# Layer 0 of a two-layer Mamba kernel: B's diagonals made on GpSimd for both units, one softplus burst a block, two conv tiles activated out of PSUM, lead times given state by state

## The chip, the cores and the metric

The kernel runs on one NeuronCore of a Trainium2 chip. The metric is the device time of one execution in microseconds (us), less is better. The engines are named as in the profile: PE is TensorE (matmuls and transposes), PEld its weight loads, DVE is VectorE, ACT is ScalarE, POOL is GpSimd, SP is SyncE, which here only issues DMAs. Each engine works through its own queue in order. An instruction at the head of a queue that waits holds up everything behind it.

## What is computed

The input `x` has the shape (2, 64, 64, 256). Layer 0 adds to it a bidirectional Mamba over rows and over columns; layer 1 adds two rounds of Mamba-2 (along both axes). Everything is fp32. The change is in layer 0 alone, whose core is this:

```python
def mamba(x, in_proj_w, conv_w, conv_b, x_proj_w, dt_w, dt_b, A_log, Dp, out_w):
    xz = x @ in_proj_w.T
    xi, z = jnp.split(xz, 2, axis=-1)
    ...
    xi = jax.nn.silu(conv(xi) + conv_b)                # depthwise, 4 taps, 512 channels
    x_dbl = xi @ x_proj_w.T
    dt, Bm, Cm = jnp.split(x_dbl, [DT_RANK, DT_RANK + D_STATE], axis=-1)   # 16, 16, 16
    dt = jax.nn.softplus(dt @ dt_w.T + dt_b)
    A = -jnp.exp(A_log)
    dA = jnp.exp(dt[..., None] * A)
    dBu = (dt * xi)[..., None] * Bm[:, :, None, :]

    def step(h, t):
        dA_t, dBu_t, C_t = t
        h = dA_t * h + dBu_t
        return (h, jnp.einsum('ndk,nk->nd', h, C_t))
    ...
    y = y + xi * Dp
    y = y * jax.nn.silu(z)
    return y @ out_w.T
```

For each of 512 channels and 16 states, `h` is a linear recurrence along a sequence of 64 positions, driven by `dt * xi` times B, and read out by a sum over the states weighted with C. It runs forwards and backwards, over the rows (`mh`) and the columns (`mv`) of the image.

## The kernel before

**Tiling.** A block is four sequences of 64 in both directions: V = 512 positions in the free dimension, with channels on the 128 partitions. There are 16 blocks an axis, two axes and two images, hence 64 blocks (`Block`). The 512 channels are two units `u` of UC = 2 tiles of 128. For each unit and each of 16 states `n`, in one turn of 32 a block:

- `decay` (L744): ACT writes exp(dt * A), two instructions of 128x512.
- `inflow` (L765): dt * x * B of this state, made in one of three ways, which the string `B_BY` (L172) picks by state:
  - G: POOL multiplies `dtx` by a row of B that a DMA has spread over all partitions (`b_row`). The decay then lies in PSUM (`ps_h`), the inflow in SBUF (`b`).
  - T: ACT scales the transposed `dtxt` by B, a column now, into `scaled` (`prepare`, L753, four instructions), and PE transposes it back into `ps_h` (eight). The decay lies in `b`.
  - P: `prepare` makes diagonal matrices of B (`diag`) from the identity, in four ACT instructions, and PE multiplies `dtxt` by them into `ps_h`, with eight matmuls.
- `scan` (L780): DVE runs the recurrence over 1024 columns, into SBUF (`prod`) if POOL makes the product with C, else in place in `ps_h`.
- `times_c` (L795): the product with C's spread row (`c_row`), on POOL for the states in `POOL_C` (L176), else on DVE.
- `add` (L805): PE transposes the product eight times, accumulating into `ps_y`, the unit's sum over states.

**Buffers.** `ps_h` has two buffers, `prod` three, `b` three, `b_row` three, `c_row` four, `scaled`, `dtxt` and `diag` one each; `ps_mm`, PSUM for all projections, conv and transposes back, has two. `ps_y` has one.

**Around the states.** For each block, PE makes the input projection (`x_proj`), the conv as four diagonal matmuls for each tile and direction (`conv`), then the projections to dt, B and C (`bc_proj`) and to dt's channels (`dt_proj`). ACT copies or activates them (`x_copy`, `conv_copy` L645, `silus` L650, `dt_softplus` L711). `bc_spread` (L664) writes B and C to DRAM and issues all the row loads of the block on SP's queue, each waiting for its buffer. `dt_x` (L718) is POOL's product dt * x, after which dt is set to a huge value at the starts of sequences, so that the decay there is 0. `y_copy`, `y_back`, `gated`, `out_proj` and `residual` finish a unit or a block.

Silu and softplus lie in other activation tables than exp, so ACT loads a table before each burst of them and another to come back.

**What sets the order.** Nothing is scheduled by a compiler: `pin` keeps the program's order on each engine. Every step has a time by hand: `STEPS0` (L40) for the steps of a block, `LEADS` (L174) for the states' steps, in hundredths of a turn. `plan` (L269) shifts the list by one period for each block, and `issue` (L282) sorts all of it and records the instructions in that order. So work for later blocks stands between the states of this one. The times only fix the order; the engines then run as their semaphores let them.

## Time and profile before

| what | us |
|---|---|
| median of 3 runs | 8563.11 |
| lowest, highest | 8562.77, 8568.54 |
| the profiled execution's own time | 8561.29 |
| its span, first to last instruction | 8559.5 |

The profile is of one execution; between its span and the time of that execution lie 1.8 us. The mean granted TensorE clock was 0.967.

Busy time of the engines by stage, from the view by windows (us of the span):

| stretch | PE | PEld | DVE | ACT | POOL |
|---|---|---|---|---|---|
| 1000 to 2000, layer 0 | 899.3 | 763.8 | 959.1 | 843.9 | 989.1 |
| 4000 to 5000, layer 0 | 900.0 | 765.9 | 962.9 | 846.0 | 993.8 |
| 6600 to 7600, layer 1 | 1000.0 | 792.0 | 727.3 | 782.5 | 721.2 |

Layer 0 takes the span up to about 6240, layer 1 the rest. A group row of the profile reads: line, engine, operation, what it writes and reads, shape, count | busy time, mean ns of one | idle time of the engine just before, and what ended it. A timeline row reads: start, duration, engine, line, operation, how many in a row, and in brackets the idle time before. Lines such as L467, L470 and L474 are those of the helpers `act`, `matmul` and `transpose`, so that groups are told apart by tile names.

### The profile page before, as it was taken

The page shows a single profiled execution, that of the slowest core. Times are in us where ns is not written, and L with a number is a line of the kernel's source. Part 1 is how long each engine was busy: PE and PEld are TensorE (multiplying, and loading weights), DVE is VectorE, ACT ScalarE, POOL GpSimd, SP SyncE. Part 2 cuts the span into 40 slices and gives each one's busy share as a digit, 9 for nine tenths or more (in the row PEclk, how much of TensorE's full clock was granted, in tenths as well). Part 3 has the DMA queues.
Part 4 walks back from the last instruction along what each step waited for, and adds up shares of the span by engine and source line. Part 5 has one row for each costly group of instructions (what it writes and reads, how often), then busy time and mean ns, then how long its engine had stood idle before and what let it go on. Part 6 is the DMA issues. An engine that isn't in the chain of part 4 may idle for free. (4 is left out here: it accounts for less than half of the span.)

```text
span 8559.5 us, 150239 instructions
## 1 busy us (share of the span) xinstructions
PE 7881.5 (92%) x55632; PEld 6562.3 (77%) x55632; DVE 7631.3 (89%) x7371; ACT 7022.7 (82%) x12082; POOL 7776.3 (91%) x4490
## 2 busy tenths in 40 slices
PE   7989999899989889999998999899889999999999
PEld 6777777777777777777777777777667777777777
DVE  7999999999999999999999999999977777777776
ACT  6888888888888888888888888888868777777776
POOL 7999999999999999999999999999967777777777
PEclk9999999999999999999999999999899999999999
DMA  4445555444445555444454444555410000000001
GB/s 152 149 148 148 145 149 149 149 148 145 148 148 147 161 150 164 147 145 149 149 148 146 151 147 148 147 147 156 146 59 1 7 4 1 9 1 1 16 31 33
DMA packets 532589, 961.24 MB, mean 112 GB/s; under 512 B 64848, under 2 KB 81744, under 8 KB 530320
## 3 DMA queue, kind: packets, MB, share of 16 engines
q1 hardware_dynamic: 522352, 930.12, 36.5%
q10 hardware_dynamic: 9504, 21.51, 0.8%
q8 instruction: 440, 7.21, 0.3%
q14 instruction: 293, 2.40, 0.1%
HBM read 928.33 MB, written 23.07 MB: 111 GB/s over the span
## 5 line engine op out<-in xcount | busy, mean ns | idle before, releaser
L768 POOL TENSOR_TENSOR b<-dtx,b_row 128x1024 f32<-128x1024 f32 x1344 | 3157.7, 2369 | 1.5 <-DVE ps_h L787 1.5
L798 POOL TENSOR_TENSOR prod<-prod,c_row 128x1024 f32<-128x1024 f32 x1088 | 2562.5, 2366 | 87.6 <-DVE prod L787 82.8
L474 PE MATMUL ps_y<-ident,prod 128*128 128x128 f32 x16384 | 2146.9, 281 | 262.5 <-POOL prod L798 138.2
L474 PEld LDWEIGHTS ps_y<-ident,prod 128*128 128x128 f32 x16384 | 1893.7, 145 | 550.4 <-POOL prod L798 285.3
L467 ACT ACTIVATE ps_h<-dt,neg_a 128x512 f32<-128x512 f32 x2688 | 1848.1, 689 | 495.9 <-DVE prod L801 402.6
L787 DVE TENSOR_TENSOR_SCAN prod<-ps_h,b 128x1024 f32<-128x1024 f32 x960 | 2164.4, 2276 | 19.3 <-POOL b L768 9.4
L787 DVE TENSOR_TENSOR_SCAN ps_h<-b,ps_h 128x1024 f32<-128x1024 f32 x576 | 1313.9, 2281 | 61.9 <-issue 32.6
L801 DVE TENSOR_TENSOR prod<-ps_h,c_row 128x1024 f32<-128x1024 f32 x960 | 1176.0, 1225 | 130.3 <-DVE ps_h L787 53.7
L467 ACT ACTIVATE scaled<-dtxt,bt 128x256 f32<-128x256 f32 x2560 | 1086.6, 495 | 238.4 <-PE ps_h L474 234.3
L962 PE MATMUL ps_mm<-xn,w_in 128*128 128x256 f32 x4608 | 1062.7, 380 | 13.4 <-DVE xn L1083 13.4
L1188 POOL TENSOR_TENSOR terms<-dta,within 128x512 f32<-128x512 f32 x512 | 524.1, 1044 | 541.6 <-DVE dta L1156 527.4
L962 PEld LDWEIGHTS ps_mm<-xn,w_in 128*128 128x128 f32 x4608 | 868.2, 191 | 128.4 <-DVE xn L1083 14.3
L467 ACT ACTIVATE b<-dt,neg_a 128x512 f32<-128x512 f32 x1408 | 929.4, 707 | 0.0
L470 PE MATMUL ps_mm<-xi,diag_w 128*128 128x256 f32 (+3 forms) x4096 | 917.9, 374 | 1.4 <-ACT dtxt L467 1.2
L474 PE MATMUL ps_h<-ident,scaled 128*128 128x128 f32 x5120 | 691.0, 279 | 245.4 <-DVE prod L787 233.1
L474 PEld LDWEIGHTS ps_h<-ident,scaled 128*128 128x128 f32 x5120 | 589.2, 144 | 396.0 <-ACT ps_h L467 302.9
L787 DVE TENSOR_TENSOR_SCAN ps_h<-ps_h,b 128x1024 f32<-128x1024 f32 x384 | 876.5, 2282 | 13.5 <-POOL b L768 6.8
L470 PEld LDWEIGHTS ps_mm<-xi,diag_w 128*128 128x128 f32 x4096 | 752.2, 190 | 80.7 <-ACT dtxt L467 3.0
L1043 DVE SCALAR_TENSOR_TENSOR conv<-ps_mm,cols,conv 128x252 f32<-128x252 f32 (+2 forms) x1536 | 705.3, 474 | 64.2 <-ACT conv L959 27.9
L470 PE MATMUL ps_mm<-xn,w_in 128*128 128x256 f32 x2048 | 549.2, 417 | 7.4 <-POOL xn L597 4.1
L1295 DVE TENSOR_TENSOR yg<-ps_mm,gate 128x512 f32<-128x512 f32 x256 | 165.0, 686 | 421.5 <-PE ps_mm L962 421.5
L959 ACT ACTIVATE conv<-ps_mm,cols 128x256 f32<-128x256 f32 x512 | 261.4, 561 | 262.8 <-PE ps_mm L962 252.6
(144 smaller groups left out, 12104.0 us busy)
## 6 DMA issues: line engine op xcount, KB each, us to landing
c_row<-bc_rows SPq DMA_DIRECT2D x2048, 256.0 KB, 3.5
b_row<-bc_rows SPq DMA_DIRECT2D x1344, 256.0 KB, 3.5
y_in<-y SPq DMA_DIRECT2D x32, 256.0 KB, 3.0
out_dram<-y_in SPq DMA_DIRECT2D x32, 256.0 KB, 2.5
XU<-in_x_dram SPq DMA_DIRECT2D x8, 512.0 KB, 7.9
bc_rows<-dbc SPq DMA_DIRECT2D x64, 64.0 KB, 3.1
XU<-in_x_dram ACTq DMA_DIRECT2D x8, 512.0 KB, 6.3
y<-Y ACTq DMA_DIRECT2D x8, 512.0 KB, 5.1
```

Of the source, the lines that this page charges most:

```text
L467: pin(nc.scalar.activation(*args, **kwargs))
L470: pin(nc.tensor.matmul(out, lhsT=lhsT, rhs=rhs, start=start, stop=stop))
L474: nc.tensor.matmul(out, lhsT=x, rhs=order, start=start, stop=stop, is_transpose=True)
L768: pin(nc.gpsimd.tensor_mul(b, self.dtx[u], self.row(u, 0, n)))
L787: nc.vector.tensor_tensor_scan(*(t.rearrange("p c t -> p (c t)") for t in (to, a, b)), 0.0, ALU.mult, ALU.add,)
L798: pin(nc.gpsimd.tensor_mul(prod, prod, self.row(u, 1, n)))
L801: pin(nc.vector.tensor_mul(prod, self.h[u, n], self.row(u, 1, n)))
L959: pin(nc.scalar.activation(*args, **kwargs))
L962: pin(nc.tensor.matmul(out, lhsT=lhsT, rhs=rhs, start=start, stop=stop))
L1043: nc.vector.scalar_tensor_tensor(dsts[:, :, j:], pps[:, :, : L - j], w[:, TAPS - 1 - j : TAPS - j], dsts[:, :, j:], ALU.mult, ALU.add,)
L1188: nc.gpsimd.tensor_mul(terms, self.dta[:, s, :].unsqueeze(2).to_broadcast([P, NH, L]), k.within.unsqueeze(1).to_broadcast([P, NH, L]),)
L1295: pin(nc.vector.tensor_mul(yg5[:, :, :, e, :], py, gate5[:, :, :, e, :]))
```

## The change

Seven things change, all in layer 0:

- `B_BY`, `POOL_C`: the states are dealt out anew. G, T, P states of a block go from 21, 10, 1 to 16, 10, 6; products with C on POOL from 17 to 20, on DVE from 15 to 12.
- `prepare` for P: one POOL instruction of 128x512 (identity times B's column, both broadcast) in place of four on ACT. It is done for unit 0 only; `diag` gets three buffers, and unit 1 uses the same diagonals again. So that it can, unit 1 takes its states in another order (`STATES`), in which states 2, 3 and 5 fall on its P places 4, 8 and 11.
- `dt_softplus`: unit and half are steps of their own, and all four stand together, before both `dt_x`; one table load there and one back. dt gets three buffers. For this the four `dt_proj` come early; dt's rows of `w_x` and `w_dt` are held twice (partitions 0 and 32), so two weight loads become four and two DMAs.
- `silus`: `xc` is two tiles of two channel tiles each (three buffers); tiles 0 and 1 go through `conv_copy` as before, tiles 2 and 3 stay in `ps_mm` until the silu reads them there, with its bias.
- `LEADS` gives six times for each unit and state in place of three for each kind, `STEPS0` and the others are given in thousandths of a turn and are all new.
- `bc_spread` writes B and C in two DMAs, and the order of the row loads on SP (`ROWS`) follows from the times at which the buffers are read.
- `yt` shares the one buffer of `scaled`.

```diff
-NX = RANK + 2 * NS0
+NX = 2 * RANK + 2 * NS0
...
-B_BY = ("GGGGTTGGGGTGGTGT", "GGGTGPGGGTGTGGTT")
-
-LEADS = {"G": (-55, None, -205), "T": (-127, -161, -95), "P": (-134, -716, -150)}
-
-POOL_C = ((0, 1, 2, 3, 7, 8, 11, 12, 15), (0, 2, 4, 6, 7, 9, 12, 13))
-POOL_OUT, POOL_SUM, SUM = 26, 249, 194
...
+STATES = tuple(range(NS0)), (0, 1, 4, 6, 2, 7, 8, 9, 3, 10, 11, 5, 12, 13, 14, 15)
...
+B_BY = ("GGPPGPTGTGTGTGGT", "TGGGPGGGPGTPTGTT")
...
+LEADS = (
+    (
+        (262, None, 226, 641, 2392, 3553),
+        (988, None, -690, 1116, 2152, 2783),
+        (1118, -5292, 153, 1524, 1614, 2150),
+        (570, -4768, 244, 620, 1942, 3524),
...
+POOL_C = ((0, 1, 3, 4, 5, 6, 8, 9, 11, 12, 13), (0, 1, 5, 6, 7, 8, 9, 13, 15))
+
+ROW_BUFS = 3, 4
...
+    (-6140, "dt_softplus", 0, 0),
+    (-6140, "dt_proj", 1, 0),
+    (-6140, "dt_softplus", 0, 1),
+    (-6140, "dt_proj", 1, 1),
+    (-6140, "dt_softplus", 1, 0),
+    (-6140, "dt_softplus", 1, 1),
+    (-2457, "dt_x", 1),
+    (-2296, "dt_x", 0),
...
+def row_order():
+
+    order = []
+    for what, bufs in enumerate(ROW_BUFS):
+        turns = [n for n in range(2 * NS0) if what or B_BY[n // NS0][n % NS0] == "G"]
+        reads = [TURN * n + LEADS[n // NS0][n % NS0][4 if what else 2] for n in turns]
+        for i, n in enumerate(turns):
+            time = reads[i - bufs] - (TURN * 2 * NS0 if i < bufs else 0)
+            order.append((time, n, what))
...
             def silus(self):
-                act(self.xc, self.xc, AF.Silu)
                 act(self.gate, self.gate, AF.Silu)
+                act(self.xc[0], self.xc[0], AF.Silu)
+                self.xc[1] = three.tile([P, UC, V], F32, name="xc")
+                for j in range(UC):
+                    c = UC + j
+                    act(self.xc[1][:, j, :], self.pc[c], AF.Silu, bias=self.w.conv_b[:, c, :])
                 pin(nc.scalar.preload_act_table_set(LOG_EXP))
...
-            def dt_softplus(self, u):
-                self.dt[u] = two.tile([P, UC, V], F32, name="dt")
-                for j in range(UC):
-                    c = UC * u + j
-                    act(self.dt[u][:, j, :], self.pd[c], AF.Softplus, bias=self.w.dt_b[:, c, :])
-                pin(nc.scalar.preload_act_table_set(LOG_EXP))
+            def dt_softplus(self, u, j):
+                if j == 0:
+                    self.dt[u] = three.tile([P, UC, V], F32, name="dt")
+                bias = self.w.dt_b[:, UC * u + j, :]
+                act(self.dt[u][:, j, :], self.pd[u, j], AF.Softplus, bias=bias)
+                if (u, j) == (1, UC - 1):
+                    pin(nc.scalar.preload_act_table_set(LOG_EXP))
...
             def prepare(self, u, n):
+                s = STATES[u][n]
                 if B_BY[u][n] == "T":
...
-                else:
-                    self.scaled[u, n] = dgp.tile([P, V // P, P], F32, name="diag")
-                    for v in range(V // P):
-                        b = self.bt[:, v, n : n + 1]
-                        act(self.scaled[u, n][:, v, :], k.ident, AF.Copy, scale=b)
+                elif u == 0:
+                    w = self.diag[s] = dgp.tile([P, V // P, P], F32, name="diag")
+                    pin(
+                        nc.gpsimd.tensor_mul(
+                            w,
+                            k.ident.unsqueeze(1).to_broadcast([P, V // P, P]),
+                            self.bt[:, :, s : s + 1].to_broadcast([P, V // P, P]),
+                        )
+                    )
...
-                w = self.scaled.pop((u, n))
+                w = self.scaled.pop((u, n)) if B_BY[u][n] == "T" else self.diag[STATES[u][n]]
```

## The prediction

> **What bounds the kernel now.** I read the page first (busy shares and the 40 slices), then the tile view of `bt` for the length of a block, then one undisturbed millisecond of layer 0 by window, by group and by wait, and last PE's timeline there. The chain on the page does not help: it ends in layer 1 and names PE for 26% of the span.

> ```profile
> PE 7881.5 (92%) x55632; PEld 6562.3 (77%) x55632; DVE 7631.3 (89%) x7371; ACT 7022.7 (82%) x12082; POOL 7776.3 (91%) x4490
> POOL 7999999999999999999999999999967777777777
> ```

> ```profile
> L467 ACT ACTIVATE bt<-ps_mm x64: 198/202/225, 58.8 to 6129.3; 128x64 f32<-128x64 f32 x64
> ```

> `b_copy` runs once a block, so a block takes (6129.3 - 58.8)/63 = 96.36 us. There are 64; they fill three quarters of the span, and layer 1 behind them isn't touched.

> ```profile
> 3000.00:4000.00 1000.00, 904.05 (x5850) 769.02 (x5849) 959.87 (x593) 846.89 (x1434) 987.98 (x475) 0.96 0.50 151
> ```

> The columns are PE, PEld, DVE, ACT, POOL, the clock, DMA. POOL is at 98.8%, DVE at 96.0%: POOL is the bound, and DVE follows.

> ```profile
> L768 POOL TENSOR_TENSOR b<-dtx,b_row 128x1024 f32<-128x1024 f32 x218 | 512.6, 2371 | 0.0
> L798 POOL TENSOR_TENSOR prod<-prod,c_row 128x1024 f32<-128x1024 f32 x177 | 417.1, 2368 | 10.8 <-DVE prod L787 10.3
> L801 DVE TENSOR_TENSOR prod<-ps_h,c_row 128x1024 f32<-128x1024 f32 x155 | 189.9, 1225 | 20.6 <-DVE ps_h L787 8.3 <-POOL b L768 3.2 <-PE ps_y L474 1.5
> L470 PE MATMUL ps_h<-diag,dtxt 128*128 128x128 f32 x176 | 22.6, 281 | 9.7 <-DVE prod L801 9.7
> ```

> The last row is the one P state of a block before: 176 records in 11 blocks are 16 for each, two for each of its 8 fp32 matmuls (transposes have one record each). PE's timeline gives the price:

> ```profile
> 3407.63 1.85 PE L470 MATMUL ps_mm<-xi,diag_w 128*128 128x256 f32 x8
> 3409.32 1.91 PE L474 MATMUL ps_y<-ident,prod 128*128 128x128 f32 x16
> 3411.07 0.38 PE L474 MATMUL ps_mm<-ident,yt 128*128 128x128 f32 x2
> 3412.40 2.05 PE L470 MATMUL ps_h<-diag,dtxt 128*128 128x128 f32 x16 [0.73 <-DVE prod L801]
> 3414.29 0.38 PE L474 MATMUL ps_mm<-ident,yt 128*128 128x128 f32 x2
> ```

> From one start to the next, a 128-column record takes 0.110 us, one of a P state (3414.29 - 3412.40)/16 = 0.118, a 256-column one 0.211.

> [...]
> - [...] The trace has 2.37, and 2.33 from start to start.
> - [...]
> - [...] The trace has 1283[...] (a load at 4005.46, its softplus at 4006.76), so a saved load is worth 1.3 us.
> - [...] I therefore count PE by start-to-start times.

> **The change by engines, per block.**
> POOL. Before, it makes 21 b tiles (G states) and 17 products; after, 16 and 20, so 38 large operations become 36: -2 x 2.33 = -4.66. Three diagonals a block are new, each one product of 128x512 with both inputs broadcast, and each serves both units, since the second unit's order of states puts 2, 3 and 5 on its P places. Before has no such row in layer 0; layer 1 has one of the same shape with the same two broadcasts:

> ```profile
> L1188 POOL TENSOR_TENSOR terms<-dta,within 128x512 f32<-128x512 f32 x512 | 524.1, 1044 | 541.6 <-DVE dta L1156 527.4
> ```

> I take 1.02 from start to start; the ends are 1.0 and 1.28 (the dense sum of L1247). 3 x 1.02 = +3.06, net -1.6 (-0.8 at the dear end). POOL's work before is 38 x 2.33 = 88.5, dtx 4.7, xn 1.1 and 1.1 for the rest (diagonals of weights, memsets): 95.4, beside 0.96 of idle. After: 93.8.
> DVE. Three products less, 15 to 12: -3 x 1.2 = -3.6. Before it is busy 0.96 x 96.36 = 92.5 us of a block, in part over queue gaps; after 89.
> ACT. Table loads go from 6 to 4 (-2.6); the diagonal's four 0.387 us copies go (-1.5); two Identity copies of 0.67 go (-1.3); the silus become 1.04 + 1.04 + 2 x 0.67 in place of 1.91 + 1.04 (+0.5). That is -5 of 81.6 busy. ACT waits 0.15 of the time now, so this is worth nothing directly.
> PE. P states rise from 1 to 6: 5 x 16 x 0.118 = +9.4. T states stay at 10. Before, the counts of a block at the dense rates are 256 adds, 80 T transposes and 68 other 128-column records at 0.11 (44.4), 64 conv at 0.211 (13.5), 64 projections of 256 columns at 0.216 (13.8), 16 records of 512 columns at about 0.5 (8.0), the P state (1.9): 81.6 of 96.36. After: 91.0, or 97% of what POOL needs. This is the risk of the change.
> DMA and SP. Five b rows of 256 KB fewer, one bc_rows write more: nothing, since SP waits for buffers and not for bandwidth. The weight loads are 4 and 2 issues in place of 1 and 1, on ACT's queue at three turns of the weights: under 1 us in all.
> Start. Both units' softplus now precede the first decay (+1.4), and dtx of unit 1 and one diagonal precede unit 0's dtx and first b (+3.4): +5 us once.

> **Where it goes around the block's turn.** POOL's order there is product 9, b of 13, diagonal, dtx 1, dtx 0, diagonal, b of the next block's state 0: about 14 us in which one b tile and one product come out. DVE is covered: states 10, 11, 12 are T or P, with 3 x 3.4 us of scans and products, then 13 on the finished b, then 14 and 15 by T. That is 18 us against 14. The softplus burst (about 5.3 us) is covered likewise: the decays of 8 to 10 stand ahead of it.
> PE is worse off. At the end of unit 0 the `skip` (3.6 us), an x_proj (1.7), dtx_back (0.9) and the T inflow of 15 (0.9) stand ahead of the add of state 11. DVE's product 14 needs the `prod` buffer which that add frees (three buffers). Following the orders through a block by hand with these durations, that product comes some 3 us later than DVE could make it, and POOL sees up to 2.4 of it later in unit 1; some of the gap is there before as well. I take the idle of POOL from 0.96 to 1.4 us: the ends are 0.3 (DVE and ACT have more room, fewer late scans) and 3.4.

> **Sum.** 93.8 + 1.4 = 95.2 a block, -1.15 x 64 = -74, +5 at the start: -69. The profiled execution took 8561.3 us (its span 8559.5), so 8492; the median of before lies 1.8 higher: 8494.

> **Rivals.**
> B: POOL stays saturated as before, the idle doesn't grow: -1.6 x 64 + 5 = -97, 8466. For it: DVE and ACT both get looser. Against it: PE.
> C, slower: PE's queue decides. Place: the six P inflows. Each waits at PE's head for its PSUM pair (0.9 us for the P state now, 9.7 us in 11), and everything behind it waits as well, above all the adds that free `prod`. Price: the 2.4 us above, all on POOL, making 93.8 + 0.96 + 2.4 = 97.2, +0.84 x 64 + 5 = +59: 8622. It decides from 1.6 us of new POOL idle a block. For it: 91.0 of PE work in 95, in order. Against it: PE's 9.3 us of idle a block are mostly waits for products it is early for, which a fuller PE absorbs.
> D: the two cancel, 8546 to 8580. The change not doing what it says would show as softplus loads still at 6 a block; the order of the built program has one burst, so I give that nothing.

> **Chances.** Forecast 0.50 (its own range 8440 to 8545), B 0.13, C 0.27, D 0.10. This measurement can tell 0.2%, some 17 us. Faster 0.63, same 0.10, slower 0.27. The range 8430 to 8620 leaves out about half of C and a little of B's far side.

> **What would show it.** The spacing of the `bt` copies: 95.2 if right, 94.7 under B, over 96.4 under C. The diag row on POOL: 192 of 1.04 us. The products on POOL, 1280 with idle before them near 1.4 us a block; 1024 b tiles. P matmuls 6144 records; PE busy over 95% in a layer 0 window; DVE's products waiting for PE ps_y, few in the forecast and 2 us a block or more in C. The forecast is wrong if POOL's busy share falls below 97% in layer 0, or the diagonals cost over 1.5 us each.

## The result and the profile after

| kernel | median us | runs | lowest, highest |
|---|---|---|---|
| before | 8562.15 | 12 | 8552.84, 8572.70 |
| after | 8555.22 | 12 | 8538.43, 8575.31 |

The ratio is 0.9992, with a 95% interval of 0.9983 to 1.0001: no difference that can be measured, where 8494 had been forecast. The profiled execution took 8556.71 us, its span 8555.0.

First the page of after, the same part as was shown of before (busy time, share of the span, instructions):

```profile
PE 8252.8 (96%) x60752; PEld 7001.7 (82%) x60752; DVE 7426.6 (87%) x7179; ACT 6732.7 (79%) x11698; POOL 7670.7 (90%) x4554
```

The work moved as the diff says: DVE lost 204.7 us, ACT 290.0, POOL 105.6, and PE gained 371.3. The length of a block, from the tile view of `bt`, hardly changed: (6118.7 - 60.6)/63 = 96.16 us, against 96.36.

```profile
L531 ACT ACTIVATE bt<-ps_mm x64: 202/204/224, 60.6 to 6118.7; 128x64 f32<-128x64 f32 x64
```

The window of one millisecond of layer 0 (columns PE, PEld, DVE, ACT, POOL, clock, DMA) says more:

```profile
3000.00:4000.00 1000.00, 967.02 (x6652) 840.06 (x6651) 922.92 (x560) 796.48 (x1364) 965.88 (x484) 0.98 0.45 138
```

POOL's share fell from 98.8% to 96.6%, below the 97% at which the forecast had called itself wrong. POOL has less to do and waits for somebody. The view of POOL's waits in layer 0 (who waits, for whom: us in total, times, longest) gives, for before and then for after:

```profile
POOL prod L798 <- DVE prod L787: 72.3, 72, 4.1
POOL prod L798 <- DMA XU<-y: 2.4, 1, 2.4
POOL b L768 <- DVE ps_h L787: 1.5, 4, 0.4
```

```profile
POOL b L849 <- DVE prod L868: 127.4, 56, 6.6
POOL prod L879 <- DVE prod L868: 17.3, 16, 2.3
POOL b L849 <- DVE ps_h L868: 6.6, 4, 2.3
POOL b L849 <- DMA XU<-y: 5.0, 1, 5.0
POOL b L849 <- DMA c_row<-bc_rows: 3.7, 3, 1.3
POOL b L849 <- DMA XU<-in_x_dram: 1.8, 1, 1.8
```

Together 76 us before and 162 after. A new wait stands first: a b tile that waits for a scan, 56 times in 62 blocks, so once in nearly every block. POOL's timeline has it at the turn of the block, right after dtx 1, dtx 0 and the diagonal: it is the b tile of the next block's state 0, and it needs the `b` buffer that the scan of state 13 of unit 1 still reads. Here are two successive ones (start, duration, ..., idle before and its releaser):

```profile
3442.00 2.36 POOL L849 TENSOR_TENSOR b<-dtx,b_row 128x1024 f32<-128x1024 f32 x1 [1.34 <-DVE prod L868]
3539.26 2.36 POOL L849 TENSOR_TENSOR b<-dtx,b_row 128x1024 f32<-128x1024 f32 x1 [4.62 <-DVE prod L868]
```

The length is not the same each time, and the blocks aren't either. I took the length of all 63 blocks from the starts of POOL's dtx. Most blocks of after take 94.0 to 94.7 us, but 18 of them 97 or more. Five of these stand at the start and at changes of stage (100.1 to 116.0; before has such blocks too), the other 13 anywhere. The median block went from 95.54 to 94.64, a gain of 0.90, and the mean only from 96.46 to 96.21. The 13 blocks are what the median doesn't see.

The block of the second row above is one of the 13. PE's clock tells it apart (windows of 2 us of after, columns as before):

```profile
3518.00:3520.00 2.00, 2.00 (x11) 1.03 (x9) 1.80 (x2) 1.89 (x3) 2.00 (x2) 0.91 0.85 267
3520.00:3522.00 2.00, 2.00 (x10) 1.67 (x11) 1.39 (x2) 0.59 (x1) 2.00 (x2) 0.50 0.28 92
3522.00:3524.00 2.00, 2.00 (x6) 0.50 (x5) 2.00 (x1) 0.20 (x1) 2.00 (x2) 0.50 0.35 129
3524.00:3526.00 2.00, 2.00 (x10) 1.91 (x9) 0.33 (x2) 1.98 (x3) 2.00 (x2) 0.50 0.37 131
3526.00:3528.00 2.00, 2.00 (x11) 1.75 (x10) 0.99 (x1) 1.81 (x4) 2.00 (x2) 0.88 0.34 129
```

For some 6.8 us PE runs at half its clock, and these lie in the turn, as the timeline of after shows for the same stretch:

```profile
3518.70 1.17 PE L534 MATMUL ps_mm<-dbc,w_dt 16*128 16x512 f32 x2
...
3519.80 1.97 PE L538 MATMUL ps_h<-ident,scaled 128*128 128x128 f32 x8
...
3521.69 2.08 PE L534 MATMUL ps_mm<-dbc,w_dt 16*128 16x512 f32 x4
...
3523.70 1.97 PE L538 MATMUL ps_y<-ident,prod 128*128 128x128 f32 x8
3523.80 1.27 ACT L531 ACTIVATE dt<-ps_mm,cols 128x512 f32<-128x512 f32 x2 [3.21 <-PE ps_mm L534]
...
3525.76 1.23 DVE L882 TENSOR_TENSOR prod<-ps_h,c_row 128x1024 f32<-128x1024 f32 x1 [1.67 <-PE ps_y L538]
...
3529.75 2.30 DVE L868 TENSOR_TENSOR_SCAN ps_h<-b,ps_h 128x1024 f32<-128x1024 f32 x1 [2.76 <-ACT scaled L531]
```

The block before, at full clock, has these rows in the same place:

```profile
3425.68 1.09 PE L538 MATMUL ps_h<-ident,scaled 128*128 128x128 f32 x8
3426.70 1.13 PE L534 MATMUL ps_mm<-dbc,w_dt 16*128 16x512 f32 x4
3427.86 1.27 ACT L531 ACTIVATE dt<-ps_mm,cols 128x512 f32<-128x512 f32 x2 [1.39 <-PE ps_mm L534]
3428.68 1.91 PE L534 MATMUL ps_mm<-xn,w_in 128*128 128x256 f32 x8
3430.43 1.95 PE L534 MATMUL ps_h<-diag,dtxt 128*128 128x128 f32 x16
3432.48 2.30 DVE L868 TENSOR_TENSOR_SCAN ps_h<-b,ps_h 128x1024 f32<-128x1024 f32 x1 [1.75 <-PE ps_h L534]
```

Eight transposes take 1.97 us in place of 1.09, the four records of dt's projection 2.08 in place of 1.13. The second half of the softplus burst on ACT waits 3.21 for them (1.39 in the block before), the decay behind it is late, DVE's scans 11 to 13 are late, and POOL gets 4.62 us of idle in place of 1.34. It is one chain through four engines: PE, ACT, DVE, POOL. All of the 13 blocks have such a stretch in the turn that they begin with, and apart from the five at the start and the stage changes no other block has.

The half clock itself is not new. Between 100 and 6300 us (layer 0 and the change to layer 1), the 2-us windows add up to 544 us of it in before and to 211 in after. Nor was it free in before. Here is a stretch of before in the same columns, POOL fifth:

```profile
3426.00:3430.00 4.00, 4.00 (x14) 2.07 (x13) 3.84 (x4) 3.21 (x8) 3.95 (x3) 0.50 0.57 196
3430.00:3434.00 4.00, 4.00 (x12) 2.17 (x11) 3.15 (x2) 2.86 (x4) 4.00 (x2) 0.50 0.40 106
3434.00:3438.00 4.00, 4.00 (x21) 4.00 (x20) 0.86 (x1) 3.75 (x7) 4.00 (x3) 0.50 0.46 156
```

POOL works through these windows, but the wait comes just behind them. The last transposes at half clock are late, DVE waits for them, and POOL for DVE:

```profile
3435.12 1.91 PE L474 MATMUL ps_h<-ident,scaled 128*128 128x128 f32 x8
3437.14 2.30 DVE L787 TENSOR_TENSOR_SCAN ps_h<-b,ps_h 128x1024 f32<-128x1024 f32 x1 [3.91 <-PE ps_h L474]
3442.97 4.69 POOL L798 TENSOR_TENSOR prod<-prod,c_row 128x1024 f32<-128x1024 f32 x2 [3.86 <-DVE prod L787]
```

Away from the start and the stage changes, four blocks of before begin with such a long stretch, and they take 98.2 to 98.6 us. In six others the only stretch of the first 80 us is a short one of 3.4 us, some 38 us into the block; POOL waits nowhere in these, and they take 94.3 to 94.4. Most of the rest have a stretch of 6.8 us some 14 us into the block and a wait of POOL of up to 1 us. So POOL's waits in before go with the half clock too. This is a reading of the trace; no run takes the half clock out of before.

That gave two theories of the lost gain: it went to the half clock at the turn (the clock theory), or to the order at the turn whatever the clock (the loop theory: softplus burst, P inflow of state 11 behind an x_proj, scans 11 to 13, b). The rivals of the forecast stayed as well: PE's amount of work, and POOL alone.

### The profile page after: what moved, and what is told of

It reads as the page before. It is cut to its first block, busy times and chain, and to the rows that moved or that the text cites. A ratio compares the mean times of both kernels' runs of the same rounds, so it can differ in the third digit from the quotient of the medians.

```text
span 8555.0 us, 159111 instructions
## 1 busy us (share of the span) xinstructions
PE 8252.8 (96%) x60752; PEld 7001.7 (82%) x60752; DVE 7426.6 (87%) x7179; ACT 6732.7 (79%) x11698; POOL 7670.7 (90%) x4554
## 5 line engine op out<-in xcount | busy, mean ns | idle before, releaser
L879 POOL TENSOR_TENSOR prod<-prod,c_row 128x1024 f32<-128x1024 f32 x1280 | 3008.8, 2375 | 42.2 <-DVE prod L868 38.7
L849 POOL TENSOR_TENSOR b<-dtx,b_row 128x1024 f32<-128x1024 f32 x1024 | 2420.2, 2378 | 148.9 <-DVE prod L868 131.0
L531 ACT ACTIVATE ps_h<-dt,neg_a 128x512 f32<-128x512 f32 x2048 | 1410.1, 689 | 532.0 <-DVE prod L882 408.4
L868 DVE TENSOR_TENSOR_SCAN prod<-ps_h,b 128x1024 f32<-128x1024 f32 x768 | 1731.0, 2274 | 59.3 <-POOL b L849 34.8
L531 ACT ACTIVATE b<-dt,neg_a 128x512 f32<-128x512 f32 x2048 | 1357.1, 711 | 81.7 <-DVE prod L868 78.3
L868 DVE TENSOR_TENSOR_SCAN ps_h<-b,ps_h 128x1024 f32<-128x1024 f32 x512 | 1170.1, 2285 | 142.5 <-PE ps_h L534 90.6
L868 DVE TENSOR_TENSOR_SCAN prod<-b,ps_h 128x1024 f32<-128x1024 f32 x512 | 1166.8, 2279 | 62.8 <-PE ps_h L538 35.6
L1036 PE MATMUL ps_mm<-xn,w_in 128*128 128x256 f32 x4608 | 1062.7, 380 | 13.2 <-DVE xn L1157 13.2
L534 PE MATMUL ps_h<-diag,dtxt 128*128 128x128 f32 x6144 | 768.6, 279 | 90.7 <-DVE prod L882 61.3
L534 PEld LDWEIGHTS ps_h<-diag,dtxt 128*128 128x128 f32 x6144 | 728.7, 193 | 135.0 <-ACT ps_h L531 75.5
L868 DVE TENSOR_TENSOR_SCAN ps_h<-ps_h,b 128x1024 f32<-128x1024 f32 x256 | 583.2, 2278 | 0.2 <-ACT ps_h L531 0.2
```

Source lines behind the costliest of these rows:

```text
L531: pin(nc.scalar.activation(*args, **kwargs))
L534: pin(nc.tensor.matmul(out, lhsT=lhsT, rhs=rhs, start=start, stop=stop))
L849: pin(nc.gpsimd.tensor_mul(b, self.dtx[u], self.row(u, 0, n)))
L868: nc.vector.tensor_tensor_scan(*(t.rearrange("p c t -> p (c t)") for t in (to, a, b)), 0.0, ALU.mult, ALU.add,)
L879: pin(nc.gpsimd.tensor_mul(prod, prod, self.row(u, 1, n)))
L1036: pin(nc.tensor.matmul(out, lhsT=lhsT, rhs=rhs, start=start, stop=stop))
```

## The experiments

Each kernel is the one after the change with one edit, where nothing else is said. Ratios are against the kernel before; the change itself has 0.9992.

**The b tile ahead of the decay at the turn.** Recorded ahead of decay 15, the b tile of the next state 0 takes the buffer of state 12, which comes free earlier. No engine's own order changes.

```diff
+                    if (u, n, name) == (0, 0, "inflow"):
+                        lead = -450
                     if lead is not None:
```

> The changed kernel with one order altered: the b tile of the next block's state 0 is recorded ahead of the decay of state 15, so that it takes the buffer of state 12 and not that of state 13; no engine's own order changes. Theory T (the gain on POOL's work was given back in one wait at the turn of the block, 1.35 us in every block and 4.6 us where PE's clock is halved there, 149 us in all): the idle before the b tiles falls from 149 us to under 50, and the time to 8455 (8430 to 8480). Rival P (PE, 96.7% busy, is the bound, and the wait only shows it): POOL's idle goes to other rows and the time stays within 0.3% of 8555. Rival K (the halved clock sets the time): the waits of 1.35 us go, those of 4.6 stay in part, 8480 to 8510.

Measured: 8533.06 (6 runs), ratio 0.9965 [0.9954, 0.9976]. POOL's waits in layer 0 are now these:

```profile
POOL prod L879 <- DVE prod L868: 106.3, 107, 2.3
POOL b L849 <- DVE ps_h L868: 30.8, 20, 2.8
POOL b L849 <- DVE prod L868: 2.2, 2, 1.1
```

The wait at the turn is gone (127.4 to 2.2), yet most of it comes back as waits of products for the same late scans: 140 us in all, against 162. The median block is 94.23. A wait taken from POOL at one place is no gain if the scans it waits for remain late. 12 blocks still take 97 or more.

**dt's projection over 64 rows.** The half-clock stretches begin around the matmuls of 16 rows, so these get 64 (weights of the others zero).

```diff
-                rows = slice(32 * j, 32 * j + RANK)
+                rows = slice(0, NX)
```

> The changed kernel with dt_proj's matmuls over 64 partitions (dt's weights, with zeros in the rows of B, C and the second dt) in place of 16; their number, their columns and their results are the same. Rival K: [...] the halved stretches there go (from about 15 in layer 0 to a few), the mean clock rises from 0.987 to over 0.993, and the time falls by 0.43 us for each us at half clock less, some 40 us, to 8515. Theory T and rival P: if rows don't count for the clock, nothing changes, 8555 within 15.

Measured: 8556.44 (13 runs), 0.9993 [0.9984, 1.0001]. The half clock at the turns is gone (92 us left between 100 and 6300 us, at the stage changes and behind the last block), and so are the 97-us blocks in between; but now most blocks take 94.9 to 95.7 and wait 2.25 us at the turn. The timeline of this kernel shows the reason in the one row

```profile
3429.01 1.98 PE L534 MATMUL ps_mm<-dbc,w_dt 64*128 64x512 f32 x4
```

against 1.13 for the four records of 16 rows. In after the two halves use different rows (0 to 15 and 32 to 47), and their records start together, at 3426.70 in the rows of the undisturbed block above; over 64 rows the four take 0.85 us longer. The edit cured one thing and broke another: these 0.85 us in the chain became 0.9 us of POOL's wait.

**Decay 11 of unit 1 ahead of the softplus burst, and x_proj 0 behind inflow 11.** If the order at the turn is the bound, the scan 11 should come sooner.

```diff
-        (29, None, 289, 2125, 2175, 4103),
+        (-1150, None, 289, 2125, 2175, 4103),
...
-    (-36767, "x_proj", 0),
+    (-36700, "x_proj", 0),
```

> The changed kernel with the decay of unit 1's state 11 ahead of the softplus burst, and the projection x_proj 0 behind the P inflow of state 11 on PE. Theory T says that the scan of state 13 is late because DVE waits 1.75 us (2.8 where the clock is halved) before the scan of state 11, for these two: the wait of 1.35 us on POOL goes, 8470 (8440 to 8500). Rival P: PE has the same work, so the wait turns up in other places, 8555 within 25. Rival K: like P in blocks at half clock, so 8490 to 8530.

Measured: 8771.68, 1.0245 [1.0231, 1.0259]; POOL's wait for the b buffer grew to 326 us, 5.5 a block. The decay put forward writes a `b` tile itself, and the softplus burst stands behind it on ACT; that it waits there for a buffer, and the burst with it, is the author's estimate and was not shown. The expectation fell.

**No skip matmuls.** Is it PE's amount of work?

```diff
-                for v in range(V // P):
+                for v in range(0):
```

> The changed kernel without the 32 skip matmuls' records of each block (xi times D is left out of y): PE has 3.6 us less work a block, nothing else changes. Rival P: the time falls by 1.5 to 3.6 us a block, to 8330 to 8460. Theory T: the skips stand elsewhere than the turn's chain (softplus, decay and inflow of 11, three scans), so the wait there stays and the time falls by less than 30 us, to 8530 to 8555; it may even rise if the clock is halved more often.

Measured: 8611.7, 1.006 [1.004, 1.008]. Taking 3.6 us of PE away made it slower. Undisturbed blocks stay at 94.0 to 94.1 (94.6 over the columns, as in after), but the half clock rises from 211 to 299 us and POOL's wait at the turn from 127 to 171. So PE's amount of work isn't what holds an undisturbed block; with less for PE to do, its half clock took more time.

**Less POOL work, in mid-block and at the turn.** Three of POOL's 20 products a block cover one channel tile of two, 1.1 us less each by the trace (1.27 against 2.37): in unit 0's states 5, 8 and 12, or in unit 1's states 7, 8 and 9, just ahead of the turn.

```diff
+                    if (u, n) in ((0, 5), (0, 8), (0, 12)):
+                        half = self.spread[u, 1, n].to_broadcast([P, 1, V])
+                        pin(nc.gpsimd.tensor_mul(prod[:, 0:1, :], prod[:, 0:1, :], half))
+                    else:
+                        pin(nc.gpsimd.tensor_mul(prod, prod, self.row(u, 1, n)))
```

> The changed kernel with POOL's product with C done for one of the two channel tiles alone in states 5, 8 and 12 of unit 0 (the other half goes into the sum without C): 3.5 us less POOL work a block, all between the turn's wait and POOL's b tiles of unit 1. Loop theory (the period is one round: POOL's work from the b tile of the next block's state 0 to the b tiles of 5 to 7 of unit 1, then DVE, ACT and PE through the softplus burst and the scans of 11 to 13, back to that b tile): all of it shortens the round, unless DVE or PE bind there: 90.6 to 92 us a block, 8340 to 8440. Rival P (PE's 90 us of work bind everywhere): under 1 us a block, 8490 to 8555.

> The same saving of 3.5 us of POOL work a block, in states 7, 8 and 9 of unit 1, whose products stand on POOL just ahead of the turn. Loop theory: POOL is only waiting there, so its wait for the scan of state 13 grows by 3.5 us a block (to some 4.8 in undisturbed blocks) and the time stays within 25 us of 8555. Plain POOL theory (POOL's work and one fixed wait sum up): the same gain as in the run before, 8340 to 8440.

Measured: 8527.21, 0.9957 [0.9943, 0.997] in mid-block, 8562.09, 1.0004 [0.9995, 1.0012] at the turn. At the turn POOL simply waits longer for the scan, as the loop theory had it:

```profile
POOL b L849 <- DVE prod L868: 301.5, 61, 9.5
```

In mid-block that theory expected 8340 to 8440, and failed: of some 3.3 us a block only 0.4 to 0.5 came out (undisturbed blocks over the rows 94.0 to 93.6, over the columns 94.6 to 94.1). POOL's waits, nearly all of them for DVE's scans, rose from 162 to 337 us. So even away from the turn POOL has hardly a lead over DVE.

**Less DVE work in mid-block.** The same for three of DVE's own products.

```diff
+                    if (u, n) in ((0, 7), (0, 10), (0, 14)):
+                        half = self.spread[u, 1, n].to_broadcast([P, 1, V])
+                        pin(nc.vector.tensor_mul(prod[:, 0:1, :], self.h[u, n][:, 0:1, :], half))
```

> DVE's products of unit 0, states 7, 10 and 14 cover one channel tile of two (the other half of the product is left as it lies, so y is not the reference's): about 0.6 us less each, 1.8 us of DVE a block, POOL unchanged. Theory that the blocks now go through DVE's chain of scans as much as through POOL (94.0 of which DVE is busy 89 and waits for PE 3): undisturbed blocks fall to about 93, POOL's wait of 1.35 us at the turn nearly vanishes, time 8480 to 8510. Theory that POOL is the bound in all but the turn: 8550 to 8560. Theory that PE's order holds the block: also about 8550, with DVE's waits for PE longer by the 1.8.

Measured: 8535.76 (7 runs), 0.997 [0.996, 0.9981]; median block 94.20. The products took 0.69 in place of 1.22, 1.6 us a block, of which little came out: undisturbed blocks over the rows stay at 94.0, those over the columns fall from 94.6 to 94.1. The time lies between the expectations. Undisturbed, the block is held within half a microsecond by POOL and by DVE with its waits for PE; relieving either alone is worth half a microsecond at most.

**The swap and the later x_proj.**

> The order of b tiles as in e1_bswap, and x_proj 0 recorded behind the P inflow of state 11 of unit 1, so that PE makes this inflow 1.7 us earlier. Loop theory: the scan of state 11 then waits for its decay on ACT in place of the inflow, 0.6 us earlier; where POOL no longer waits at the turn this is room and little time: 8500 to 8530, and fewer long waits where the clock is halved. Rival P: no change from e1_bswap's 8533 within 8.

Measured: 8563.43 (13 runs), 1.0000 [0.9992, 1.0009]. The swap's gain is lost again. ACT's copies of the projection into `xi`, 8 us of waiting for PE in after, now wait 77 us, and what stands behind them on ACT comes after them. That this is the whole cause was not tried.

**dt's projection over 32 rows.** The cure of the clock without the damage: each half takes the rows that lie next to it, with zero weights, so that the halves use rows 0 to 31 and 32 to 63.

```diff
-                self.w_dt = wp.tile([3 * RANK, DI], F32, name="w_dt")
+                self.w_dt = wp.tile([NX, DI], F32, name="w_dt")
+                pin(nc.gpsimd.memset(self.w_dt, 0.0))
...
-                rows = slice(32 * j, 32 * j + RANK)
+                rows = slice(32 * j, 32 * j + 2 * RANK)
```

> The delta projection's four matmuls a block take 32 rows each in place of 16 (the weights of the 16 rows added are zero, so nothing of the result changes); the two row groups can still run side by side, which the 64 rows of the earlier run could not (its four records took 1.98 us, against 1.13). Clock theory (PE's clock halves for some 6.8 us where transposes and the narrow matmuls follow each other at the turn, and since the change the turn can no longer absorb it; a block hit so costs 97.3 in place of 94.0 to 94.6): the half-clock stretches at the turns go, the share of blocks at 97 or more falls from 19 in 63 to the few at the sequence boundaries, mean 95.5, time 8500 to 8520. If the halving is not set by the rows, or does not cost the time: 8550 to 8560, as the change itself.

Measured: 8511.21 (8509.58 to 8511.36), 0.9942 [0.9929, 0.9956]: inside what the clock theory gave. In the timeline of this kernel, two turns of POOL and the projection between them, the four records still take 1.13 us, and the wait at the turn is the short one both times.

```profile
3420.07 2.38 POOL L850 TENSOR_TENSOR b<-dtx,b_row 128x1024 f32<-128x1024 f32 x1 [1.32 <-DVE prod L869]
...
3498.88 1.13 PE L534 MATMUL ps_mm<-dbc,w_dt 32*128 32x512 f32 x4
...
3514.18 2.37 POOL L850 TENSOR_TENSOR b<-dtx,b_row 128x1024 f32<-128x1024 f32 x1 [1.34 <-DVE prod L869]
```

Its window of the same millisecond has the full clock, and POOL back at 98.3%:

```profile
3000.00:4000.00 1000.00, 966.02 (x6765) 841.48 (x6764) 934.57 (x567) 807.97 (x1387) 983.10 (x495) 1.00 0.45 139
```

All 13 blocks of 97 us are gone, while the median block is the same (94.58 against 94.64); the 63 blocks together take 6014.0 us, 47 less than in after. The runs tell it too: those of after spread over 37 us, these over 2.

**Both: 32 rows and the swap.**

> The same, together with the b tile of the next block's state 0 recorded ahead of decay 15 (the edit that gave 8533). Clock theory, where both costs are separate: 8480 to 8500, undisturbed blocks at 93.6 to 94.2. If the swap had its gain only from fewer halved stretches: no better than the 32 rows alone.

Measured: 8489.15 (8487.84 to 8489.49), 0.9917 [0.9903, 0.9931]. The two costs are separate, and this kernel beats both. Its median block is 94.20, and of POOL's waits in layer 0 these are left, 93.5 us, 1.5 a block:

```profile
POOL prod L880 <- DVE prod L869: 83.8, 84, 2.5
POOL b L850 <- DVE ps_h L869: 7.5, 5, 2.3
POOL b L850 <- DVE prod L869: 2.2, 2, 1.1
```

**The kernel before, with 48 rows.** A control: is the half clock free where POOL is the bound?

```diff
-                self.w_dt = self.load(wp, [RANK, DI], "w_dt", d[self.m + "_dt_w"])
+                self.w_dt = wp.tile([NX, DI], F32, name="w_dt")
+                pin(nc.gpsimd.memset(self.w_dt, 0.0))
+                pin(self.dma.dma_start(out=self.w_dt[0:RANK, :], in_=d[self.m + "_dt_w"]))
...
-                    self.pd[c], self.w.w_dt[:, c * P : (c + 1) * P], self.dbc[:RANK, :], True, True
+                    self.pd[c], self.w.w_dt[:, c * P : (c + 1) * P], self.dbc[:NX, :], True, True
```

> The control for the clock: the kernel before the change, its delta projection's four matmuls a block over 48 rows in place of 16 (the weights of the 32 rows added are zero; in this kernel the four already run one after the other, so no concurrency is lost). Its trace shows 544 us of half clock in layer 0, more than the 211 after the change. Clock theory (before, PE stood idle 9 us a block and POOL set the period, so that the half clock was absorbed; after, PE has 3 us left): half-clock stretches become fewer, the time stays within 15 us of before. If the half clock cost time before too, and the change merely inherited it: 8520 to 8540, and then it explains nothing of why the gain did not come.

Measured: 8580.85 (14 runs), 1.0021 [1.0013, 1.0029]. It is no control: the half clock didn't go (560 us against 544). The last section has what goes with it: in before, 60 of 73 drops of the clock follow 3.41 us in which PE is busy for less than 1.8, and with the wider matmuls it is 59 of 73. The 17 us come from the edit itself. At each change of the weights `w_dt` is now cleared on POOL, ACT issues the DMA into it, and waits at the head of its queue until POOL has come to it, three times for 9.5 to 10.0 us:

```profile
1556.10 1.71 ACT L467 ACTIVATE scaled<-dtxt,bt 128x256 f32<-128x256 f32 x4 [10.01 <-POOL w_dt L519]
```

The three blocks that this hits take 107.0 to 108.4 us, against 99.6 to 100.0 in before, which is more than the whole loss. So no run tests what the half clock cost in before; the trace says that it did cost (shown with the result).

**32 rows, the swap, and the diagonal of state 5 earlier.**

```diff
-        (-947, -4106, 14,
+        (-947, -4800, 14,
```

> The 32 rows and the swap, and besides the decay of unit 0's state 5 due earlier (lead -4800 in place of -4106), which puts the diagonals of state 5 and what follows from them on POOL's and ACT's queues ahead of their neighbours. Theory that POOL, now 98.6% busy in layer 0, is again what sets the block, so that only a shift of single waits is left: within 10 us of 8489. If the order around state 5 still costs a wait in each block (POOL's products wait for DVE's scans 84 us in all): 8430 to 8470.

Measured: 8489.15, 0.9912 [0.9898, 0.9926]: the same as without it.

## Why the prediction was wrong

| kernel | median us | mean block | median block | blocks of 97 or more | POOL's waits, 100 to 6100 |
|---|---|---|---|---|---|
| before | 8562.15 | 96.46 | 95.54 | 15 | 76 |
| after | 8555.22 | 96.21 | 94.64 | 18 | 162 |
| swap | 8533.06 | 95.89 | 94.23 | 12 | 140 |
| 32 rows | 8511.21 | 95.46 | 94.58 | 5 | 115 |
| 32 rows, swap | 8489.15 | 95.13 | 94.20 | 6 | 94 |

**POOL's work: right.** The diagonals are 192 and take 1.04 to 1.05 us; products are 1280, b tiles 1024:

```profile
L839 POOL TENSOR_TENSOR diag<-ident,bt x192: 1037/1050/1182, 60.9 to 6144.4; 128x512 f32<-128x512 f32 x192
```

For the rest I take the 50 blocks away from the start and the stage changes, and split the mean length of each kernel's block into POOL's waits in it and what is left:

| kernel | mean of the 50 blocks | POOL's waits | without the waits |
|---|---|---|---|
| before | 95.44 | 0.82 | 94.63 |
| after | 95.34 | 2.39 | 92.94 |
| swap | 94.81 | 1.82 | 92.99 |
| 32 rows | 94.41 | 1.42 | 92.98 |
| 32 rows, swap | 94.00 | 1.00 | 93.00 |

POOL's work fell by 1.69 us a block, where 1.6 was forecast.

**DVE, ACT and PE in amount: right.** DVE's 204.7 us less are 3.2 a block (3.6 forecast), ACT's 290.0 are 4.5 (5). A P state at full clock takes 0.112 us a record, so the five new ones cost 9.0 (9.4). The forecast left the lengths of POOL's and DVE's large instructions as they were. That was the author's estimate, and the window from 3000 to 4000 us bears it out: POOL's b tile takes 2371 ns before and 2376 after, its product 2368 and 2374, DVE's product 1225 in both. A table load on ACT takes 1283 ns in both; between 100 and 6100 us they fell from 374 to 248.

**"Where it goes around the block's turn": the step that failed.** It said "DVE is covered", 18 us of scans against 14 of POOL, and "The softplus burst (about 5.3 us) is covered likewise", and took POOL's idle from 0.96 to 1.4 us a block. So it asked whether DVE would run out of work during POOL's stretch of dtx and diagonals. It did not ask whether POOL would then find a free buffer for its next b tile, and put that wait at nothing. Measured, the waits rose by 1.57 us a block, and took back nearly all of the 1.69.

What the change added is this wait at the turn, for the b buffer that the scan of state 13 still holds. With the half clock out of the turn (32 rows) it stands alone, 1.42 us a block. Counting durations, scan 13 would have been done by then; but DVE waits 1.75 us at scan 11 for its P inflow, which stands on PE behind an x_proj (`ps_mm<-xn,w_in` at 3428.68 and the inflow `ps_h<-diag,dtxt` at 3430.43 in the rows of the undisturbed block above). The prediction saw an x_proj in the way at the end of unit 0, not here. The swap takes this wait away, yet 1.00 us of waits for late scans remains, so it brings 22 us and not the whole.

The other 0.97 us of the 2.39 is the half clock, which adds some 3.3 us or more to each turn that it hits. The prediction read all of PE's prices at full clock in one undisturbed stretch, though the window that it quotes has 0.96 in the clock's column. But this cost is mostly an old one: before has 0.82 us of waits a block, and they go with the half clock there. The prediction carried them along in its 0.96 without knowing what they were. Taking the half clock out of the turn brings 47 us over the 63 blocks (44 in the median time); it is a gain beyond what the change was to bring, and not the gain that was lost.

In sum: -1.69 of work, +1.42 at the turn, and +0.15 of half clock give -0.12 us a block; the table has -0.10. That the kernel with both mended comes to 8489, beside 8494 forecast, is luck in part: the forecast left most of before's waits in place, and this kernel has lost those and has others.

**The rivals.** B (idle unchanged) falls with the waits. C named PE's queue, and priced it through all six P inflows and the adds that free `prod`: of the inflows one, that of state 11, shows in DVE's waits; DVE's products waiting for PE's `ps_y` rose only from 16.5 to 39.3 us in layer 0, 0.4 a block, not the 2 that C needed; and with less PE work the time rose. D, the two cancel, had the outcome, with no mechanism to name. The forecast's own sign for being wrong, POOL under 97%, was met.

**What stays open:** why the product waits of about 1 us a block in the best kernel resist, and what before would gain from a full clock.

## What to carry to other kernels

When an engine near its limit is relieved, go through its remaining work at the place where it bunches up, and ask of each operation which buffer it needs and who still holds it: here one wait of 1.42 us a block took back most of 1.69 us saved. Split the block into work and waits in both kernels before a cost is called new: a half clock that disturbs the new kernel may have disturbed the old one as much. Look at the blocks one by one: a median that gains and a mean that doesn't points to a disturbance in some of them, and a wide spread between runs to the same (37 us in after, 2 with 32 rows). And a wait removed at one place pays only if what it waited for is no longer late.

## What the runs showed of the hardware

In before the drops go with idleness, though PE is not wholly idle: of 73 drops between 100 and 6100 us, 60 follow a step in which PE is busy for less than 1.8 of 3.41 us. With 48 rows in this kernel it is 59 of 73, so most drops come in the same way there. In after idleness is not all: 13 of 23 drops follow a step in which PE is busy for 3.35 us or more. Ahead of the turn shown it was 3.39 of 3.41 us, filled with transposes and the matmuls of 16 rows. With 32 rows in each of two groups, at the same 1.13 us, the stretches at the turns don't occur, between 3030 and 4530 us not one, against seven stretches in after. So in this kernel they go with the 16 rows; why was not shown.

Which turns are hit goes with where the grid lies. In after a turn is hit when a point of the grid falls 8.6 to 9.3 us ahead of POOL's first dtx. In the turn shown this point is 3519.65, and the step that ends there holds the first two of the four matmuls of dt's projection, which start at 3516.65 and 3518.70. Of the turns that are not hit, only two at the very edge of this range, and those next to the start and to stage changes, have a point there. In before the blocks can keep step with the grid: twelve in a row, 1694 to 2841 us, take 95.57 us on average, the length of 28 steps (95.57), with the stretch 13.9 to 14.2 us into each. Which of the two sets the other was not shown.

Among the 12 runs of after, time and the mean clock of the run go together: 8538.43 us at a clock of 0.990, 8575.31 at 0.985. And two matmuls of 16 or 32 rows run side by side in these kernels when their rows are different ones: with 16 rows four records of two halves take 1.13 us, and two of one half alone 1.12 (3424.62 in after); with 32 rows it is 1.13 and 1.12 (3498.88 and 3496.81 in the run with 32 rows). Where the four take 64 rows, or the same 16 rows (before, at 3475.39), they last 1.98.
